# Cross-attention and FFN in one kernel: the maxima's short key chunk moved out of the key loop and rewritten as four full-array matmuls

## The chip, the core and the metric

The program runs on one core of one Trainium2 chip. The metric is the device time of one execution in microseconds. TensorE is called PE (PEld for its weight loads), VectorE DVE, ScalarE ACT, GpSimd POOL and SyncE SP, as in the profile. Two kinds of float are used on PE: float32, whose matmul stands in the trace as two instructions (two passes), and the rounded float32r, with one.

## The reference

A block with cross-attention and a feed-forward network, batch 1, everything in float32:

```python
x = x + xattn(layernorm(x), ctx)      # 2048 rows of 256; ctx 1601 rows of 192
#   q = layer_norm(x, g) @ Wq         # 16 heads of 64
#   k, v = split(ctx @ Wkv); a learned null key and value is put in front: 1602 keys
#   attn = softmax(mask(q k^T / 8)); out = layer_norm((attn v) @ Wout, g_out)
x = x + ffn(layernorm(x))             # 256 -> 1024 -> 1024 -> 256, weights +-1, relu
```

## The kernel before, in words

The attention is cut into 32 units `(p, b)`: a pair `p` of heads (8 of them, two heads of 64 fill the 128 partitions) and a block `b` of 512 query rows (4). The order of all instructions on every engine is the program's order; it is written by hand (`manual_schedule`), and nothing is moved by a scheduler. Buffers come from rings: a new tile of a ring takes the place of the one allocated so many allocations earlier, and its first writer waits for that one's last reader.

Two rings hold PSUM. `spare` (tag "s", two buffers) holds the scores of the even and the odd key tile, the weighted sum `av` and the output projection `po`. `flex` (tag "f", two buffers) holds the maxima's products, the denominators `den`, the turned maxima `mt`, and the projections of queries, keys and values (`psq`, `psk`, `psv`).

The softmax needs a row maximum before the exponentials are taken. It is computed from rounded copies: `qr` and `kr` are float32r copies of the queries `qT` and keys `kT`. A unit's maxima are found one unit ahead, in `max_chunk(p, b, n)`: for each of 4 query tiles of 128 rows there are three wide chunks of 512 keys (n = 0 to 11), each two matmuls, one for each head on its 64 rows of the array (L400) and one DVE reduction over both (L403). The keys 1536 to 1601, 66 of them, are the short chunk, `REST` (n = 12): for all four query tiles and both heads eight matmuls of 66 columns on 64 rows (L384) and one reduction (L387) into column 3 of the tile `mx`.

One unit in the order of PE:

1. The loop over 13 key tiles. Step k: `exps` issues the scores of tile k (two float32 matmuls on 64 rows each, four instructions, L442), for k below 2 also the matmul that adds the shift (L466), and ACT takes the exponential (L468) into the tile `e`; then one chunk of the next unit's maxima. The chunks go in the order 0 to 10, REST, 11, so REST is in step 11. POOL adds up the `e` tiles into `acc` for the denominators (L720, L722, L728).
2. `den`: the denominators of the unit before (L499; in 28 of the units ahead of the weighted sum, in units 1, 30 and 31 within it, in unit 0 not at all), whose reciprocal (L511) and copies (L517, ACT) give `aoT`.
3. The weighted sum `av`, 13 times four matmuls with 32 columns of weights (L475), copied to `avs` by ACT (L782).
4. The projections: `mt` (L413) turns the next unit's maxima, DVE makes the shift `mT` of them (L415); `po` is the output projection of the unit before (L488), added to `y_sb` by DVE (L493); `psq` the queries two units ahead (L211), copied by ACT to `qr` and `qT` (L212, L213); then, for seven pairs out of eight, a half of the next pair's keys (`project_k`, L270 and L275, in b = 0 and 1) or values (`project_v`, L305 and L320, in b = 2 and 3). DVE makes `kT` of the key projection (L232), ACT rounds it to `kr` (`round_k`, L289, ahead of `avs`), and copies the values (L329).

The prologue computes the first pair's keys, values and the maxima of unit (0, 0), with POOL rounding the keys; its REST comes after the query projection of unit (0, 1). After the attention the feed-forward part follows; its first block starts beside the last unit.

Of the kernel before, what the change touches and what calls it, by code (L numbers as in the profile page):

```python
# [31 lines left out]
REST = 12  # L32
# [6 lines left out]
def xattn_ffn(ctx, tc, x, ctxT, mask, g_norm, null_kv, wq, wkv, wout, g_out, k0, k1, k2, s0, s1, s2, out):  # L39
# [9 lines left out]
    def flex(name):  # L49
        return ps_f.tile([128, 2, 512], F32, tag="f", name=name)  # L50
# [97 lines left out]
    with ExitStack() as att:  # L148
# [15 lines left out]
        spent = ap.tile([128, 1], F32, name="spent")  # L164
        ones_r = ap.tile([128, 128], F32R, name="ones_r")
        mcol = ap.tile([128, 128], F32, name="mcol")
        pick = ap.tile([128, 4, 1], F32, name="pick")

        weights = {}
# [25 lines left out]
        def project_q(p, b, get=flex, part=None):  # L195

            if part is not None:
                if part == 0:
                    halves["q"] = get(f"psq_{p}_{b}")
                ps = halves["q"]  # L200
                nc.tensor.matmul(
                    ps[:, 0, :], weights[p][0][:, part, :], xnT[:, b, part, :], start=part == 0, stop=part == 1
                )
                if part == 0:
                    return
            qT = wp.tile([128, 512], F32, tag="qT", name=f"qT_{p}_{b}")
            qr = wp.tile([128, 512], F32R, tag="qr", name=f"qr_{p}_{b}", bufs=1)
            if part is None:
                ps = get(f"psq_{p}_{b}")
            for c in range(2) if part is None else ():  # L210
                nc.tensor.matmul(ps[:, 0, :], weights[p][0][:, c, :], xnT[:, b, c, :], start=c == 0, stop=c == 1)  # L211
            nc.scalar.mul(qr, ps[:, 0, :], DH**-0.5)  # L212
            nc.scalar.mul(qT, ps[:, 0, :], DH**-0.5)  # L213
            queries[p, b] = (qT, qr)
# [19 lines left out]
        def first_keys(n, get, part=None):  # L234

            kT, _, kr = pairs[0]
            chunks = (CHUNKS[1], CHUNKS[2]) if n == 1 else (CHUNKS[n],)
            if part != 1:
                halves["k"] = get(f"psk_0_{n}")
            ps = halves["k"]  # L240
            for i, (start, w) in enumerate(chunks):
                if part is None or part == i:
                    nc.tensor.matmul(
                        ps[:, i, :w], weights[0][1][:, 0, :], ctx_a[:, ds(start, w)], start=True, stop=False
                    )
            if part == 0:
                return
            for i, (start, w) in enumerate(chunks):
                rows = ts(i, 64)
                nc.tensor.matmul(  # L250
                    ps[:, i, :w], weights[0][2][rows, 0, :], ctx_b[rows, ds(start, w)], start=False, stop=True
                )
            for i, (start, w) in enumerate(chunks):
                for part in range(2 if n == 0 else 1):
                    keys = ds(256 * part, 256) if n == 0 else ds(start, w)
                    relative(kT, ps[:, i, ts(part, 256)] if n == 0 else ps[:, i, :w], keys)
                    if n == 0 and part == 0:
                        nc.scalar.copy(kr[:, keys], kT[:, keys])
                    else:
                        nc.gpsimd.tensor_copy(kr[:, keys], kT[:, keys])  # L260
            if n == 3:
                nc.vector.memset(kT[:, KEYS:], 0.0)

        def project_k(p, m):

            kT = pairs[p][0]
            start, w = HALF_KEYS[m]
            ps = flex(f"psk_{p}_{m}")
            for i in range(2):
                nc.tensor.matmul(  # L270
                    ps[:, i, :w], weights[p][1][:, 0, :], ctx_a[:, ds(start + i * w, w)], start=True, stop=False
                )
            for i in range(2):
                rows = ts(i, 64)
                nc.tensor.matmul(  # L275
                    ps[:, i, :w], weights[p][2][rows, 0, :], ctx_b[rows, ds(start + i * w, w)], start=False, stop=True
                )

            for i in range(2):
                relative(kT, ps[:, i, :w], ds(start + i * w, w))  # L280
            if m == 1:
                nc.vector.memset(kT[:, KEYS:], 0.0)

        def round_k(p, m):

            kT, _, kr = pairs[p]
            start, w = HALF_KEYS[m]
            keys = ds(start, 2 * w)
            nc.scalar.copy(kr[:, keys], kT[:, keys])  # L289

        def keys_stepped(p):

# [83 lines left out]
        def max_chunk(p, b, n, get=flex):  # L376
            ps = get(f"max_{p}_{b}_{n}")
            qr, kr = queries[p, b][1], pairs[p][2]
            if n == REST:
                start, w = CHUNKS[3]  # L380
                for t in range(4):
                    for j in range(2):
                        rows = ts(j, DH)
                        nc.tensor.matmul(  # L384
                            ps[:, j, ts(t, w)], qr[rows, ts(t, 128)], kr[rows, ds(start, w)], start=True, stop=True
                        )
                nc.vector.tensor_reduce(  # L387
                    maxima[p, b][:, :, :, 3].rearrange("p t j -> p j t"),
                    ps[:, :, : 4 * w].rearrange("p j (t k) -> p j t k", k=w),
                    AX.X,  # L390
                    ALU.max,
                )
                return
            t, c = divmod(n, 3)
            if n == 0:
                maxima[p, b] = wp.tile([128, 4, 2, 4], F32, tag="mx", name=f"mx_{p}_{b}")
            start, w = CHUNKS[c]
            for j in range(2):
                rows = ts(j, DH)
                nc.tensor.matmul(  # L400
                    ps[:, j, :w], qr[rows, ts(t, 128)], kr[rows, ds(start, w)], start=True, stop=True
                )
            nc.vector.tensor_reduce(maxima[p, b][:, t, :, c], ps[:, :, :w], AX.X, ALU.max)  # L403
# [33 lines left out]
        def scores(p, b, k, ps):  # L437
            kT, qT = pairs[p][0], queries[p, b][0]
            n = rows_of(k)
            for j in range(2):  # L440
                rows = ts(j, DH)
                nc.tensor.matmul(  # L442
                    ps[:n, j, :],
                    kT[rows, ds(128 * KEY_TILES[k], n)],
                    qT[rows, :],
                    start=k < 2,
                    stop=k >= 2,
                    skip_group_check=k >= 2,
                )
# [111 lines left out]
                nc.vector.tensor_scalar_mul(xnT[:, b, 1, :], pts[1][:, 1, :], gn_sb[:, 1:2])  # L561

        units = [(p, b) for p in range(NP) for b in range(NB)]
        order = (*range(REST - 1), REST, REST - 1)

        begin = tc.manual_schedule()
        begin.__enter__()
# [51 lines left out]
        for j in range(2):  # L619
            nc.gpsimd.dma_start(out=nullv[:, ts(j, DH)], in_=null_kv[1:2, :])  # L620
        nc.gpsimd.memset(mcol, 0.0)
        nc.gpsimd.memset(kept, 0.0)
        nc.gpsimd.tensor_scalar(ones_r, ident, 0.0, 1.0, ALU.mult, ALU.add)
        nc.gpsimd.tensor_tensor(pick[:, :, 0], ident[:, 0:4], ident[:, DH : DH + 4], ALU.add)
# [41 lines left out]
        input_turned(1, spare)  # L666
        max_chunk(0, 0, 8)
        max_chunk(0, 0, 11)
        project_q(0, 1, spare)
        max_chunk(0, 0, REST)  # L670
        odd = spare("sT_0_0_1")
        sT = [spare("sT_0_0_0"), odd]
        scores(0, 0, 1, sT[1])
        max_combined(0, 0)
        max_turned(0, 0)
        scores(0, 0, 0, sT[0])
        masked_counted(flex)
        begin.__exit__(None, None, None)
        last = None
        with tc.manual_schedule():  # L680
            for u, (p, b) in enumerate(units):
# [27 lines left out]
                for k in range(KC):  # L709
                    if k == (2 if 2 < u < len(units) - 4 else 8) and last is not None:  # L710
                        nc.scalar.copy(seen[:, 1:2], last[3][:1, 0, 0:1])
                    if k == 0 and u > 0:

                        odd = spare(f"sT_{p}_{b}_1")
                        sT = [spare(f"sT_{p}_{b}_0"), odd]
                    es.append(exps(p, b, k, sT))
                    if nxt is not None:
                        max_chunk(*nxt, order[k])
                    if k == 2:
                        nc.gpsimd.tensor_tensor(acc, es[1], es[2], ALU.add)  # L720
                    elif 2 < k < 8:
                        nc.gpsimd.tensor_tensor(acc, acc, es[k], ALU.add)  # L722
# [64 lines left out]
                    max_turned(*nxt)  # L787
                if nxt is None:
                    uT = turned(0)
                if last is not None:  # L790
                    project_out(*last[:2], aoT)
                if u + 2 < len(units):
                    project_q(*units[u + 2])
                if p + 1 < NP:

                    (project_k if b < 2 else project_v)(p + 1, b % 2)
                    if b == 2:
                        keys_stepped(p + 1)
                last = (p, b, avs, acc)
# [154 lines left out]
```

## Time and profile before

| What | Value |
|---|---|
| median of 3 runs (lowest to highest) | 1270.56 us (1269.84 to 1270.65) |
| the profiled execution's own time | 1270.18 us |
| its span | 1268.4 us |
| granted TensorE clock | 1.00 |
| wide chunk's reduction on DVE, L403, 384 of them | 1218 ns each |
| exponential on ACT, L468, 416 of them | 1024 ns each |
| wide chunk's matmuls on PE, L400 | 280.6 us busy |
| short chunk's matmuls on PE, L384 | 29.6 us busy |
| weighted sum on PE, L475 | 363.6 us busy |
| PE in one unit's loop, 399.1 to 413.3 us of the span | 14.20 us busy of 14.20 |

The first exponentials of most units follow each other after 32.85 us (33.5 where a unit projects the first half of the values, 31.2, 31.0 and 30.0 in the last pair). Times are those of one execution; the profile numbers lines by kernel.py. Single records of the trace are meant where a time has three digits after the point.

### The profile page before, as it was taken

To read this page: it belongs to the slowest core of one execution; us is meant where nothing else is said; L and a number is where in the kernel's file an instruction comes from. 1 tells how busy PE (TensorE), PEld (TensorE's weight loads), DVE (VectorE), ACT (ScalarE), POOL (GpSimd) and SP (SyncE) were. 2 spreads that over 40 slices of the span, in tenths; PEclk is the share of its full clock that TensorE was granted. 3 is DMA by queue.
4 is the path that set the end of the run, shared out by engine and by line. 5 is a ranking of instruction groups with operands and counts; after the bars stand their busy time and mean duration, and the time that the engine had idled before them with its cause. 6 is when DMAs were issued, how large, how long until landed. Compare 5 with 4: busy or idle time off the path is not lost.

```text
span 1268.4 us, 19642 instructions
## 1 busy us (share of the span) xinstructions
PE 1257.9 (99%) x8332; PEld 644.0 (51%) x8332; DVE 761.7 (60%) x812; ACT 717.9 (57%) x982; POOL 1008.5 (80%) x515
## 2 busy tenths in 40 slices
PE   8999999999999999999999999999999999999998
PEld 5344444444444444444444444444444443788887
DVE  6687766656665566556655666656666793635431
ACT  4776666666666656665666566666666676322120
POOL 5898999899889988998899988998898999701100
PEclk9999999999999999999999999999999999999999
DMA  6000000000000000000000000000000010000000
GB/s 171 1 1 5 1 1 13 5 1 1 13 5 1 1 14 5 1 1 13 5 1 2 13 5 1 1 1 6 1 17 1 1 42 1 1 17 1 17 17 17
DMA packets 16984, 13.46 MB, mean 11 GB/s; under 512 B 3152, under 2 KB 16336, under 8 KB 16896
## 3 DMA queue, kind: packets, MB, share of 16 engines
q1 hardware_dynamic: 15904, 11.21, 3.2%
q8 instruction: 65, 1.06, 0.4%
q10 hardware_dynamic: 656, 0.79, 0.2%
q0 software_dynamic: 336, 0.21, 0.1%
q14 instruction: 23, 0.19, 0.0%
HBM read 10.11 MB, written 2.10 MB: 10 GB/s over the span
## 4 chain that ended last, share of the span: by engine, by line
PE 95%; POOL 2%; ACT 1%; DMA 1%; issue 0%; DVE 0%; SPq 0%; DVEq 0%; POOLq 0%; ACTq 0%
PE sT L442 28%; PE av L475 27%; PE ps L836 12%; PE max L400 7%; PE psq L211 4%; PE po L488 4%; PE ps L867 2%; PE psv L305 2%; PE psk L270 1%; PE den L499 1%; PE sT L466 1%; PE psv L320 1%; POOL acc L728 1%; PE psk L275 1%; PE max L384 1%; PE mt L413 1%
## 5 line engine op out<-in xcount | busy, mean ns | idle before, releaser
L403 DVE TENSOR_REDUCE mx<-max 128x2 f32<-128x1024 f32 x384 | 444.4, 1218 | 86.0 <-PE max L400 82.3
L728 POOL TENSOR_TENSOR acc<-acc,e 128x1024 f32<-128x1024 f32 x192 | 473.1, 2464 | 15.1
L468 ACT ACTIVATE e<-sT 128x1024 f32<-128x1024 f32 x416 | 425.8, 1024 | 87.7 <-PE sT L466 44.3
L442 PE MATMUL sT<-qT,kT 64*128 64x512 f32 x1664 | 444.8, 608 | 1.6 <-ACT e L468 1.3
L722 POOL TENSOR_TENSOR acc<-acc,e 128x1024 f32<-128x1024 f32 x160 | 379.3, 2371 | 12.6
L475 PE MATMUL av<-e,v 128*32 128x512 f32 x3328 | 363.6, 592 | 0.1
L400 PE MATMUL max<-kr,qr 64*128 64x512 f32 x768 | 280.6, 718 | 1.2 <-ACT qr L227 1.0
L475 PEld LDWEIGHTS av<-e,v 128*32 128x32 f32 x3328 | 107.4, 110 | 237.9 <-issue 230.1
L442 PEld LDWEIGHTS sT<-qT,kT 64*128 64x128 f32 x1664 | 134.0, 185 | 132.6 <-ACT e L468 121.0
L720 POOL TENSOR_TENSOR acc<-e,e 128x1024 f32<-128x1024 f32 x32 | 75.6, 2363 | 59.6 <-ACT e L468 59.6
L400 PEld LDWEIGHTS max<-kr,qr 64*128 64x128 f32 x768 | 76.7, 187 | 88.6 <-DVE mx L403 65.2
L517 ACT COPY aoT<-r 32x256 f32<-32x256 f32 x224 | 90.2, 403 | 33.4 <-DVE r L511 31.1
L782 ACT COPY avs<-av 128x512 f32<-128x512 f32 x32 | 18.8, 587 | 145.8 <-PE av L475 145.8
L415 DVE TENSOR_TENSOR mT<-mt,pick 128x512 fp32r<-128x512 f32 x32 | 22.1, 690 | 113.4 <-PE mt L413 112.9
L518 DVE TENSOR_TENSOR aoT<-avs,aoT 128x512 f32<-128x512 f32 x28 | 33.3, 1189 | 94.4 <-ACT aoT L517 94.4
L836 PE MATMUL ps<-h0hi,w 128*128 128x512 f32 x256 | 79.6, 392 | 0.0
L836 PE MATMUL ps<-h0lo,w 128*128 128x512 f32 x256 | 78.9, 389 | 0.0
L124 POOL TENSOR_TENSOR y_sb<-y_sb,gout_sb 128x256 f32<-128x256 f32 x12 | 9.3, 777 | 85.6 <-DVE y_sb L91 85.6
L824 ACT ACTIVATE h1hi<-ps 128x1024 fp32r<-128x1024 f32 x16 | 16.4, 1027 | 99.2 <-PE ps L836 99.2
L212 ACT ACTIVATE qr<-psq 128x512 fp32r<-128x512 f32 x31 | 18.5, 598 | 93.5 <-PE psq L211 91.4
L488 PE MATMUL po<-wo,aoT 128*128 128x256 f32 x256 | 60.5, 379 | 0.0
L825 DVE SCALAR_TENSOR_TENSOR h1lo<-ps,h1hi 128x1024 fp32r<-128x1024 f32 x16 | 19.6, 1224 | 67.0 <-ACT h1hi L824 67.0
(171 smaller groups left out, 1207.8 us busy)
## 6 DMA issues: line engine op xcount, KB each, us to landing
out_x<-o SPq DMA_DIRECT2D x7, 256.0 KB, 2.1
x_sb<-in_x SPq DMA_DIRECT2D x3, 512.0 KB, 5.2
wa<-in_wkv SPq DMA_DIRECT2D x8, 128.0 KB, 2.9
wb<-in_wkv SPq DMA_DIRECT2D x16, 64.0 KB, 2.5
wq<-in_wq SPq DMA_DIRECT2D x8, 128.0 KB, 2.2
wo<-in_wout SPq DMA_DIRECT2D x8, 128.0 KB, 2.1
xnT<-in_k SPq DMA_DIRECT2D x1, 1024.0 KB, 5.7
ctx_a<-in_ctxT SPq DMA_DIRECT2D x2, 256.0 KB, 6.2
```

Of the source, the lines that this page charges most:

```text
L211: nc.tensor.matmul(ps[:, 0, :], weights[p][0][:, c, :], xnT[:, b, c, :], start=c == 0, stop=c == 1)
L400: nc.tensor.matmul(ps[:, j, :w], qr[rows, ts(t, 128)], kr[rows, ds(start, w)], start=True, stop=True)
L403: nc.vector.tensor_reduce(maxima[p, b][:, t, :, c], ps[:, :, :w], AX.X, ALU.max)
L442: nc.tensor.matmul(ps[:n, j, :], kT[rows, ds(128 * KEY_TILES[k], n)], qT[rows, :], start=k < 2, stop=k >= 2, skip_group_check=k >= 2,)
L468: nc.scalar.activation(e, ps, AF.Exp)
L475: nc.tensor.matmul(av[ts(i, 32), 0, :], v[:n, KEY_TILES[k], ts(i, 32)], e[:n, i // 2, :], start=k == 1, stop=k == 0, tile_position=(0, 32 ...
L488: nc.tensor.matmul(pv[:, t, :], aoT[:, ts(t, 128)], weights[p][3], start=True, stop=True)
L517: nc.scalar.copy(aoT[ds(64 * j + 32 * rows, 32), ts(h, 256)], r[ds(64 * j + 32 * h, 32), :])
L720: nc.gpsimd.tensor_tensor(acc, es[1], es[2], ALU.add)
L722: nc.gpsimd.tensor_tensor(acc, acc, es[k], ALU.add)
L728: nc.gpsimd.tensor_tensor(acc, acc, es[k], ALU.add)
L836: nc.tensor.matmul(ps[:, f, :], w(c)[:, ts(2 * g + f, 128)], parts[part][:, c, :], start=i == 0, stop=i == len(steps) - 1,)
```

## The change

REST is computed differently and elsewhere. The last 66 keys of the two heads are kept apart in a tile of their own, block-diagonal: head 0's in rows 0 to 63 of the first 66 columns, head 1's in rows 64 to 127 of the other 66, zeros elsewhere. One matmul on the whole array then gives both heads' products for a query tile, 132 columns, and four do the work of the eight. Two such tiles, one for even and one for odd pairs, are zeroed once by POOL; ACT fills them after `round_k` (POOL in the prologue), with two copies of 64x66, and `round_k` leaves those keys out.

REST of unit u + 2 now stands at the end of unit u, behind the query projection that it needs, and the reduction of it with it; the prologue does it for the first two units. From unit 2 on, the query projection is put ahead of the output projection, and REST behind the latter; in units 0 and 1 REST stands between the two parts of the key projection. In the loop, step 1 has no maxima any more, and steps 2 to 12 have the chunks 1 to 11 (step 0 keeps chunk 0).

```diff
+        apart = [ap.tile([128, 2, KEYS - CHUNKS[3][0]], F32R, name=f"apart_{i}") for i in range(2)]
...
             start, w = HALF_KEYS[m]
-            keys = ds(start, 2 * w)
+            keys = slice(start, min(start + 2 * w, CHUNKS[3][0]))
             nc.scalar.copy(kr[:, keys], kT[:, keys])
+            if m == 1:
+                keys_apart(p, nc.scalar.copy)
+
+        def keys_apart(p, copy):
+
+            start, w = CHUNKS[3]
+            for j in range(2):
+                copy(apart[p % 2][ts(j, DH), j, :], pairs[p][0][ts(j, DH), ds(start, w)])
...
             if n == REST:
-                start, w = CHUNKS[3]
+                w = 2 * CHUNKS[3][1]
                 for t in range(4):
-                    for j in range(2):
-                        rows = ts(j, DH)
-                        nc.tensor.matmul(
-                            ps[:, j, ts(t, w)], qr[rows, ts(t, 128)], kr[rows, ds(start, w)], start=True, stop=True
-                        )
+                    nc.tensor.matmul(
+                        ps[:, t // 2, ts(t % 2, w)],
+                        qr[:, ts(t, 128)],
+                        apart[p % 2].rearrange("p j k -> p (j k)"),
+                        start=True,
+                        stop=True,
+                    )
                 nc.vector.tensor_reduce(
-                    maxima[p, b][:, :, :, 3].rearrange("p t j -> p j t"),
-                    ps[:, :, : 4 * w].rearrange("p j (t k) -> p j t k", k=w),
+                    maxima[p, b].rearrange("p (i t) j c -> p i (t j) c", i=2)[:, :, :, 3],
+                    ps[:, :, : 2 * w].rearrange("p i (t k) -> p i t k", k=w // 2),
...
+        for i in range(2):
+            nc.gpsimd.memset(apart[i].bitcast(F32), 0.0)
...
         max_chunk(0, 0, 11)
+        max_chunk(0, 0, REST)
         project_q(0, 1, spare)
-        max_chunk(0, 0, REST)
...
         max_turned(0, 0)
+        max_chunk(0, 1, REST)
         scores(0, 0, 0, sT[0])
...
                     es.append(exps(p, b, k, sT))
-                    if nxt is not None:
-                        max_chunk(*nxt, order[k])
+                    if nxt is not None and k != 1:
+                        max_chunk(*nxt, max(k - 1, 0))
...
+                if u >= 2 and u + 2 < len(units):
+                    project_q(*units[u + 2])
                 if last is not None:
                     project_out(*last[:2], aoT)
-                if u + 2 < len(units):
+                if u < 2:
                     project_q(*units[u + 2])
+                if u + 2 < len(units) and u >= 2:
+                    max_chunk(*units[u + 2], REST)
                 if p + 1 < NP:
 
-                    (project_k if b < 2 else project_v)(p + 1, b % 2)
+                    if u < 2:
+                        project_k(p + 1, b, 0)
+                        max_chunk(*units[u + 2], REST)
+                        project_k(p + 1, b, 1)
+                    else:
+                        (project_k if b < 2 else project_v)(p + 1, b % 2)
```

The remaining lines split `project_k` into the two parts named above and, in the prologue's `first_keys`, replace POOL's one rounding copy of the last keys by `keys_apart(0, nc.gpsimd.tensor_copy)`.

More of the change, by code (lines that the diff above doesn't have):

```diff
@@ L256, in first_keys @@
                     relative(kT, ps[:, i, ts(part, 256)] if n == 0 else ps[:, i, :w], keys)
-                    if n == 0 and part == 0:
+                    if n == 3:
+                        keys_apart(0, nc.gpsimd.tensor_copy)
+                    elif n == 0 and part == 0:
                         nc.scalar.copy(kr[:, keys], kT[:, keys])
@@ L262, in first_keys, with project_k @@
                 nc.vector.memset(kT[:, KEYS:], 0.0)
-        def project_k(p, m):
+        def project_k(p, m, part=None):
             kT = pairs[p][0]
             start, w = HALF_KEYS[m]
-            ps = flex(f"psk_{p}_{m}")
-            for i in range(2):
+            if part != 1:
+                halves["k"] = flex(f"psk_{p}_{m}")
+            ps = halves["k"]
+            for i in range(2) if part != 1 else ():
                 nc.tensor.matmul(
@@ L272, in project_k @@
                 )
+            if part == 0:
+                return
             for i in range(2):
@@ L378, in max_chunk @@
             qr, kr = queries[p, b][1], pairs[p][2]
+            if (p, b) not in maxima:
+                maxima[p, b] = wp.tile([128, 4, 2, 4], F32, tag="mx", name=f"mx_{p}_{b}")
             if n == REST:
-                start, w = CHUNKS[3]
+                w = 2 * CHUNKS[3][1]
                 for t in range(4):
-                    for j in range(2):
-                        rows = ts(j, DH)
-                        nc.tensor.matmul(
-                            ps[:, j, ts(t, w)], qr[rows, ts(t, 128)], kr[rows, ds(start, w)], start=True, stop=True
-                        )
+                    nc.tensor.matmul(
[5 more added lines that the diff above has]
+                    )
                 nc.vector.tensor_reduce(
-                    maxima[p, b][:, :, :, 3].rearrange("p t j -> p j t"),
-                    ps[:, :, : 4 * w].rearrange("p j (t k) -> p j t k", k=w),
+                    maxima[p, b].rearrange("p (i t) j c -> p i (t j) c", i=2)[:, :, :, 3],
+                    ps[:, :, : 2 * w].rearrange("p i (t k) -> p i t k", k=w // 2),
                     AX.X,
@@ L394, in max_chunk @@
             t, c = divmod(n, 3)
-            if n == 0:
-                maxima[p, b] = wp.tile([128, 4, 2, 4], F32, tag="mx", name=f"mx_{p}_{b}")
             start, w = CHUNKS[c]
@@ L563, in xattn_ffn @@
         units = [(p, b) for p in range(NP) for b in range(NB)]
-        order = (*range(REST - 1), REST, REST - 1)
         begin = tc.manual_schedule()
```

## The prediction

> **What bounds the kernel now.** I read the page first (engine shares, the chain that ended last), then the groups by form, then the timeline around one loop end, single records of the trace where the timeline merges too much, and last the one unit that computes no maxima.
>
> ```profile
> PE 1257.9 (99%) x8332; PEld 644.0 (51%) x8332; DVE 761.7 (60%) x812; ACT 717.9 (57%) x982; POOL 1008.5 (80%) x515
> PE 95%; POOL 2%; ACT 1%; DMA 1%; issue 0%; DVE 0%; SPq 0%; DVEq 0%; POOLq 0%; ACTq 0%
> ```
>
> Of the groups by form, the two of the short chunk (instructions, then busy us and mean ns of one):
>
> ```profile
> L384 PE MATMUL max<-kr,qr 64*128 64x66 f32 x256 | 29.6, 351 | 0.0
> L387 DVE TENSOR_REDUCE mx<-max 128x8 f32<-128x528 f32 x32 | 22.7, 709 | 0.7 <-PE max L384 0.5
> ```
>
> PE never rests and carries the chain; the short chunk, REST below, is 29.6 us on PE, so that is the most that its removal could bring. PE's busy share hides waits, since a matmul's record runs through its own start-up, so starts decide:
>
> ```profile
> 409.72 1.02 PE L442 MATMUL sT<-qT,kT 64*128 64x512 f32 x4
> 410.17 0.80 PE L400 MATMUL max<-kr,qr 64*128 64x512 f32 x2
> 410.81 1.09 PE L442 MATMUL sT<-qT,kT 64*128 64x512 f32 x4
> 411.33 0.93 PE L384 MATMUL max<-kr,qr 64*128 64x66 f32 x8
> 411.73 0.42 PEld L384 LDWEIGHTS max<-kr,qr 64*128 64x128 f32 x6 [0.24 <-issue]
> 412.09 1.11 PE L442 MATMUL sT<-qT,kT 64*128 64x512 f32 x4
> 412.30 0.71 DVE L387 TENSOR_REDUCE mx<-max 128x8 f32<-128x528 f32 x1
> 412.63 0.80 PE L400 MATMUL max<-kr,qr 64*128 64x512 f32 x2
> 413.36 0.16 PEld L499 LDWEIGHTS den<-acc,ones 128*32 128x32 f32 x8 [0.56 <-issue]
> ```
>
> Steps come every 1.09 and 1.16 us by turns (409.72 to 410.81), a pair in 2.25. That pair is a latency circle over the two score buffers: exp 1.02, 0.05 until the next score's weight load, 0.11 load, two passes of 0.43, 0.21 until the next exp: 2.25. A wide maximum (0.21 of PE) fits into its slack. The unit without maxima proves it: its thirteen exps span 13.82 us, the others' 13.89.
>
> ```profile
> 1055.22 0.30 PEld L442 LDWEIGHTS sT<-qT,kT 64*128 64x128 f32 x4 [1.02 <-ACT e L468]
> 1056.20 0.30 PEld L442 LDWEIGHTS sT<-qT,kT 64*128 64x128 f32 x4 [0.69 <-ACT e L468]
> ```
>
> There, with PE free, score weights still wait for ACT. Outside the loop no such slack exists: the projections stand back to back.
>
> ```profile
> 391.74 1.89 PE L488 MATMUL po<-wo,aoT 128*128 128x256 f32 x8
> 393.47 1.88 PE L211 MATMUL psq<-xnT,wq 128*128 128x512 f32 x4
> 395.19 1.95 PE L305 MATMUL psv<-wa,ctx_a 128*128 128x128 f32 x16
> ```
>
> **The change, part by part.** The sum is against the profiled execution, 1270.18 us (span 1268.4 and 1.8 around it), which is 0.38 below the median 1270.56.
>
> *REST leaves the loop.* REST holds PE from 411.73 to the next score's real start at 412.18 (its second weight load in the single records): 0.45. A wide chunk would have released PE at 411.95 and the exp circle allows 411.97, so REST lengthens the loop by 0.21 only. ACT agrees: the last exp starts 1.305 after the one before, where the alternation gives 1.095.
>
> *The other chunks shift by a step, none at k=1.* The first key tile still carries chunk 0, so the second exp starts as before. Without a maximum at k=1 the next score could start 0.1 earlier, but its exp would stand behind ACT's previous one, which already ends back to back (starts 1.094 apart for 1.02 of work). Worth nothing. DVE, 1.131 per wide reduction back to back, gets a free step there; it does not set the loop either, so again nothing.
>
> *The denominators' buffer.* This is a wait that the diff does not name. `den` takes the flexible buffer used two allocations earlier. Before, that was REST's, whose short reduction ended at 412.30 + 0.71 = 413.01, hidden: the weights of `den` went out at 413.36, 0.11 after the last maximum left the array. After, it is a wide chunk's. Its matmuls end on PE at 412.12; DVE starts at 412.20 to 412.23 (0.06 to 0.10 later, or behind the reduction begun at 411.10), takes 1.214, ends at 413.42 to 413.44, and PE passes a semaphore 0.04 + 0.05 later: 413.53, that is 0.17 after the old start. Queued behind on PE are `den` and the whole weighted sum. So 28 units (those with `den` ahead of the weighted sum) lose 0.17 in place of gaining 0.21: +4.8. Three units (0, 1 and 30) go straight to the weighted sum and gain: -0.6. If the wait fell elsewhere the 28 would gain 5.9; I take the loss, since the order of allocation leaves no other buffer.
>
> *REST among the projections.* Four full-array matmuls of 132 columns instead of eight half-array ones of 66. The eight ran in pairs 7 ns apart, pairs 0.11 apart, with only some 0.03 of columns each: weight loads set the pace. Full-array loads of 128 columns pace alike: the value projection's matmuls (L305) come every 0.112. I take four such slots, 0.45, because loads cannot run further ahead than one and the next projection's first load joins the row. Low end: 132 columns at the 0.21 per 512 of the wide chunk, 0.055 each, 0.22. High end: the price of a float32 matmul of this width, two passes at L488's 0.216 per 256 columns, 0.22 each, 0.89; against it, the columns of the old REST took no visible time beside its loads. Nothing below zero, since no PE work is dropped there. Thirty units: +13.5, between +6.6 and +26.7.
>
> A page would make it cheaper. The Trainium skill, "TensorE: Matmul & The Clock Gate", section "Back-to-back issue gap", gives about 81 ns per matmul for a stream of load and matmul pairs at 128 columns; L305's 112 ns in this trace disagree, and the measurement decides. By the page these thirty units would cost an estimated 9.7 us and the whole sum would be about 14.6.
>
> *Query projection ahead of the output projection.* Both full-array, 1.72 and 1.73, so the exchange costs nothing, and it hides the copies of `qr` and `qT` (1.3 us after the projection ends) under `po`. Without that cover REST would wait 1.3 in each unit. `po` moves 1.7 later: its DVE addition (1.22) ends about 1.4 after it, while the score that takes its buffer comes over 1.8 after it even where no key or value projection follows. The weight DMAs that SP holds until `psq` and `po` are read move by the same 1.7, a unit ahead of use. On DVE, REST's reduction (0.71) stands between that addition and the keys' subtraction (0.63 twice), which waits for key matmuls 2.2 us long: hidden; uncovered it is 0.71 per unit with keys.
>
> *Copies.* Two 64x66 copies for each of seven pairs on ACT ahead of `avs`, where ACT idles 4.41: nothing; uncovered, 14 times 0.17 to 0.4 (smallest copy, and L517), 2 to 6 us. On POOL one more small copy (0.24) and two memsets at the start.
>
> *Prologue.* The query projection, begun at 28.76, now stands behind a REST that waits for a buffer until about 29.7; the transpose at 32.50 moves to 32.8; the second REST waits for `qr`, whose projection ended 1.4 later, and stands in front of the score begun at 32.73. The first exp (34.65) comes 0 to 1 later; I take +0.7.
>
> Sum: 13.5 + 4.8 - 0.6 + 0.7 = +18.4 on 1270.18, or 1289.0 by the median.
>
> **Rivals.** *Faster: DVE's queue sets the loop.* For it: steps of 1.127 lie within 0.004 of DVE's 1.131. Then leaving REST's reduction out of the loop saves 0.63 (0.71 less the 0.08 by which reductions overlap) against 0.45 outside: -0.18 in 30 units, 1265. Against it: the unit without maxima is no shorter, and score loads wait for ACT. It decides from the point where a loop step follows DVE's end, and no such wait shows. Equally below zero would be a load price under 0.21.
>
> *`den` does not wait.* Then +13.5 - 6.5 + 0.7 = +7.7: 1278. Against it: all 28 event records of L499 come 0.04 after the end of a reduction.
>
> *Slow columns in full-array form*, 0.89 a unit: +31.6, 1302. No row shows a short matmul of that type on the full array.
>
> *It does nothing*, REST on PE at 0.22 with `den` not waiting: +0.8, 1271.
>
> **How the numbers follow.** My forecast has 0.73 (30 times 0.40 to 0.50, 28 times 0.11 to 0.20, -0.6 and a prologue of 0 to 1: +14.5 to +21, so 1285 to 1292). `den` not waiting 0.10; slow columns 0.05; the faster rival 0.08; nothing 0.04. The range takes in the forecast's bounds and the 1278 case: 1276 to 1293, leaving out 0.17. About 0.2% (2.5 us) is what a measurement of this kernel can tell. Faster by more 0.08, same 0.04, slower 0.88.
>
> **What the profile would show.** Right: `den` loads waiting for a DVE reduction in 28 units, about 0.17 later against the last exp's old place; the last exp 1.10 after the one before; REST in slots of 0.11 between output and key or value projection; units of 32.85 near 33.5. Wrong: loop steps below 1.12; REST's slots near 0.06 or 0.22; no DVE wait at `den`; a score waiting for `po`'s addition.

## The result and the profile after

| | before | after |
|---|---|---|
| median (lowest to highest) | 1270.60 us (1269.84 to 1270.65) | 1290.09 us (1289.76 to 1290.17) |
| the profiled execution's own time, and its span | 1270.18, 1268.4 us | 1290.05, 1288.3 us |
| granted TensorE clock | 1.00 | 1.00 |

Before stands here with one more run than in the table above. The ratio is 1.015, with a 95% interval of 1.0135 to 1.0166: slower by 19.5 us.

First the page of after: busy time of each engine, and the shares of the chain that ended last.

```profile
PE 1267.3 (98%) x8204; PEld 661.0 (51%) x8204; DVE 761.7 (59%) x812; ACT 717.7 (56%) x996; POOL 1008.6 (78%) x518
PE 74%; DVE 23%; ACT 1%; DMA 1%; issue 0%; SPq 0%; DVEq 0%; POOL 0%; ACTq 0%
```

PE has 128 matmuls fewer and is busy 9.4 us longer. The new thing is DVE with 23% of the chain, where it had none. The chain itself, over one unit (start, us, what), shows where that comes from:

```profile
411.12 10.28 DVE mx L421 x9
421.40 0.14 issue
421.54 0.64 PE den L517 x8
422.18 11.16 PE av L493 x104
...
435.31 1.73 PE po L506 x8
437.04 0.40 PE max L400 x4
437.44 1.16 PE psv L321 x10
```

This must be read with care. Followed back from `den` the chain reaches a wide reduction (L421), and then the eight before it, since they stand back to back. That `den` waits for DVE is real. That the nine reductions set the pace of the loop does not follow: they start 1.131 apart (419.046, 420.177, 421.308), while the maxima's matmuls ahead of them start 1.158 and 1.095 apart by turns (418.129, 419.287, 420.382), as the exps do, and e6 below relieves DVE and gains nothing. The last line but one is REST in its new place: 0.40 of the chain, with nothing beside it.

The timeline of after at the end of the loop (start, us, engine, line, operation; in brackets the idle time before and what ended it):

```profile
420.38 0.80 PE L418 MATMUL max<-kr,qr 64*128 64x512 f32 x2
421.51 0.19 PEld L517 LDWEIGHTS den<-acc,ones 128*32 128x32 f32 x8 [0.96 <-issue]
421.54 0.64 PE L517 MATMUL den<-acc,ones 128*32 128x256 f32 x8 [0.35 <-DVE mx L421]
```

All 28 of these waits, from the answer for line L517 (us, times):

```profile
  DVE mx L421: 9.8, 28
```

In single records the reduction of chunk 10 ends at 421.392, PE's event follows at 421.431, the load at 421.507 and the first matmul of `den` at 421.537. The first exp of the unit starts at 407.371: `den` starts 14.166 after it, where before it was 13.950 (unit 11 in both). The 0.35 of idle time per wait is counted from 421.182, the end of the last maximum's record, and such ends are modelled by the profile: without a wait, the load of `den` came 0.07 ahead of that end (413.363 for 413.435 in before). So the wait is 0.43 long; 0.21 of it uses up the loop's gain, and the rest is the later start.

The groups by form show the short chunk (instructions, then busy us and mean ns of one), and after them the timeline of the projections:

```profile
L400 PE MATMUL max<-apart,qr 128*128 128x132 f32 x128 | 23.6, 306 | 1.0 <-DVE mx L421 1.0
L407 DVE TENSOR_REDUCE mx<-max 128x8 f32<-128x528 f32 x32 | 22.4, 700 | 5.3 <-PE max L400 5.3
```

```profile
433.43 1.88 PE L213 MATMUL psq<-xnT,wq 128*128 128x512 f32 x4
435.15 1.89 PE L506 MATMUL po<-wo,aoT 128*128 128x256 f32 x8
435.35 0.60 ACT L214 ACTIVATE qr<-psq 128x512 fp32r<-128x512 f32 x1 [1.37 <-PE psq L213]
...
436.69 0.75 PE L400 MATMUL max<-apart,qr 128*128 128x132 f32 x4
...
437.28 1.32 PE L321 MATMUL psv<-wa,ctx_a 128*128 128x128 f32 x10
438.22 0.70 DVE L407 TENSOR_REDUCE mx<-max 128x8 f32<-128x528 f32 x1
```

REST's busy time fell from 29.6 to 23.6 us, and the kernel is slower all the same. In single records its four matmuls start at 436.690, 436.938, 437.052 and 437.161 and the value projection at 437.277; the loads run 0.11 apart. `qr` is ready at 435.95, so nothing waits for it.

Differences between the first exps of following units put the time in its places: 1.34 us before the first exp (36.00 for 34.65), 0.36, 0.29 and 0.63 in units 0 to 2, 0.67 in each of the 25 units 3 to 27 (16.7), 0.38 and 0.59 in units 28 and 29, -0.20 in unit 30, and -0.2 behind the last first exp: 19.9, the difference of the spans. Of the 1.34, some 0.21 lies ahead of anything that the change moves (e9). In unit 28 `den` came as late before (14.335 after the first exp, now 14.319), so REST's price is left there almost alone.

### The profile page after: what moved, and what is told of

It is laid out like the page before. It is cut to its first block, busy times and chain, and to the rows that moved or that the text cites. A ratio compares the mean times of both kernels' runs of the same rounds, so it can differ in the third digit from the quotient of the medians.

```text
span 1288.3 us, 19431 instructions
## 1 busy us (share of the span) xinstructions
PE 1267.3 (98%) x8204; PEld 661.0 (51%) x8204; DVE 761.7 (59%) x812; ACT 717.7 (56%) x996; POOL 1008.6 (78%) x518
## 4 chain that ended last, share of the span: by engine, by line
PE 74%; DVE 23%; ACT 1%; DMA 1%; issue 0%; SPq 0%; DVEq 0%; POOL 0%; ACTq 0%
PE av L493 28%; DVE mx L421 22%; PE sT L460 11%; PE ps L865 11%; PE po L506 4%; PE psq L213 4%; PE ps L896 2%; PE max L418 2%; PE psv L321 2%; PE psk L276 2%; PE den L517 1%; PE sT L484 1%; PE psv L336 1%; PE max L400 1%; PE psk L283 1%; DMA x_sb<-in_x 1%
## 5 line engine op out<-in xcount | busy, mean ns | idle before, releaser
L421 DVE TENSOR_REDUCE mx<-max 128x2 f32<-128x1024 f32 x384 | 444.4, 1219 | 73.7 <-PE max L418 71.6
L418 PE MATMUL max<-kr,qr 64*128 64x512 f32 x768 | 291.6, 751 | 1.2 <-ACT qr L229 1.0
L493 PEld LDWEIGHTS av<-e,v 128*32 128x32 f32 x3328 | 127.2, 110 | 218.1 <-issue 210.8
L511 DVE TENSOR_TENSOR y_sb<-po,y_sb 128x1024 f32<-128x1024 f32 x28 | 34.3, 1224 | 68.2 <-PE po L506 68.2
```

Source lines behind the costliest of these rows:

```text
L418: nc.tensor.matmul(ps[:, j, :w], qr[rows, ts(t, 128)], kr[rows, ds(start, w)], start=True, stop=True)
L493: nc.tensor.matmul(av[ts(i, 32), 0, :], v[:n, KEY_TILES[k], ts(i, 32)], e[:n, i // 2, :], start=k == 1, stop=k == 0, tile_position=(0, 32 ...
```

## The experiments

The theory is the prediction's: REST costs its four weight loads where PE has no slack, `den` waits for the buffer of a wide chunk, and the loop gains 0.21. The rivals: DVE's queue sets the loop, the columns rather than the loads set REST's price, and the form rather than the place is to blame. Every experiment was timed in several rounds against the kernel before on the same chip, except e9.

### e1 and e2: is the wait at `den` real, and what is it worth?

```diff
-                if quarters:
-                    den = flex(f"den_{p}_{b}")[:, 0, :256]
-                    denominators(last[3], den)
-                    aoT = divided_quarters(*last[:3], den)
...
+                    if k == 2 and quarters:
+                        den = flex(f"den_{p}_{b}")[:, 0, :256]
+                        denominators(last[3], den)
+                        aoT = divided_quarters(*last[:3], den)
```

`den` goes behind the first two tiles of the weighted sum, in e1 on the kernel after, in e2 on the kernel before.

> The changed kernel with the denominators' matmuls put behind the first two key tiles of the weighted sum (as units 1, 30 and 31 have them already) instead of ahead of it; nothing else differs. Theory (in the changed kernel these matmuls stand and wait for the reduction of the last but one wide chunk): two tiles are 0.86 us of PE work and cover the wait, so 28 units lose the 0.215 by which the denominators start later than before and gain the 0.21 that the loop is shorter: 28 x 0.425 = 11.9 us less, about 1278.2, and no wait of the denominators for a reduction. Rival (the later start is a drain of the array or a later exponential, and would only move to the weighted sum): within 2 us of 1290.

> The kernel before with the same displacement of the denominators, as the control: there their buffer was the short chunk's, read early. Theory: no wait to cover, 1269.5 to 1271.5. Rival (taking the denominators off the loop's end is worth something by itself): as much faster as the other run, down to 1259.

e1: 1278.09 us, ratio 1.0059 (1.0044 to 1.0074), 12.0 below after. e2: 1270.22, ratio 0.9998 (0.9989 to 1.0007). The timeline of e1 at the end of the loop:

```profile
417.16 1.92 PE L493 MATMUL av<-e,v 128*32 128x512 f32 x16
418.90 0.61 PE L517 MATMUL den<-acc,ones 128*32 128x256 f32 x8
```

No wait of `den` for DVE is left; all idle time ahead of its line in that kernel's answer for L517 (us, times) is

```profile
  issue: 16.8, 56
```

The first load of the weighted sum, at 417.162, comes 0.071 ahead of the modelled end of the last maximum (417.233), as that of `den` did before the change. The unit takes 33.09, 0.43 less than after: the 0.215 by which `den` was late, and the 0.21 that the shorter loop now gives (28 times 0.43 is 12.0). The loop itself is as long as in after, 13.68. On the kernel before the same edit is worth nothing, so it cures only the wait that the change made.

### e3: what does REST cost in its new place?

```diff
-                for t in range(4):
+                for t in (*range(4), *range(4)):
```

On the kernel after, REST's four matmuls are issued twice into the same places; all values stay as they are.

> The changed kernel with the short chunk's four full-array matmuls issued twice into the same places (the second time gives the same values). Theory (PE takes them at the pace of weight loads, 0.11 each, in a stretch without slack): 30 x 4 x 0.112 = +13.4 and 0.5 to 0.9 in the prologue, about 1304. Rival, columns hidden and loads cheap (the 0.66 per unit that the changed kernel lost is the wait alone): +2 or less, 1290 to 1292. Rival, slow columns: +26, 1316.

1304.11 us, ratio 1.0263 (1.0246 to 1.0280): 14.0 above after, or 0.44 for each of 32 sets. Units take 33.96 (+0.44). So the price is four slots of 0.11. By the page that the prediction weighed (the Trainium skill, "TensorE: Matmul & The Clock Gate", section "Back-to-back issue gap") a set would be an estimated 0.32, and this run 1300.5; the row of the value projection was the better guide.

### e4: the new place with the old form

On the kernel after, REST stands where the change puts it, but as the eight half-array matmuls of before, reading `kr`; the tiles `apart` and their copies are left out.

```diff
-                w = 2 * CHUNKS[3][1]
+                start, w = CHUNKS[3]
...
+                    for j in range(2):
+                        rows = ts(j, DH)
+                        nc.tensor.matmul(
+                            ps[:, j, ts(t, w)], qr[rows, ts(t, 128)], kr[rows, ds(start, w)], start=True, stop=True
+                        )
```

> The changed kernel with the short chunk in its old form (eight matmuls of 66 columns on half the rows, from the rounded keys; no separate key tiles, copies and memsets) at its new place. Theory: four pairs at the pace of weight loads cost the same 0.45, and two changes between whole-array and half-array matmuls come on top, at about 0.1 each in 28 units: 1290 to 1296. Rival (the full-array form is what costs): under 1284.

1298.35 us, ratio 1.0219 (1.0204 to 1.0234): 8.3 above after, and above the range expected. Its timeline:

```profile
437.92 1.89 PE L493 MATMUL po<-wo,aoT 128*128 128x256 f32 x8
439.74 0.63 PE L391 MATMUL max<-kr,qr 64*128 64x66 f32 x8
440.31 1.38 PE L310 MATMUL psv<-wa,ctx_a 128*128 128x128 f32 x10
```

The four pairs are 0.11 apart as ever, with 66 columns where the full-array matmuls have 132, so the columns do not set that pace; but the unit is 0.31 longer (33.83 for 33.52). In single records the last matmul of `po` starts at 439.434, and REST's first weights are loaded at 439.741, 0.307 later; in after they are loaded 0.001 after that matmul's start. A gap comes back behind REST, where the last pair starts at 440.10 and the value projection's first load is at 440.305. Both loads come 0.07 ahead of the modelled end of the matmul before them (439.813 and 440.376). In all 28 units with REST behind `po` it is so, and in before at all 28 loads of `den`: where the form changes, the next weights are loaded only about when the last matmul's record ends. A change between the half array and the whole one costs 0.155 here, as the mean of the two. The Trainium skill, "TensorEngine Tiling (Array Packing)", section "Key Properties", says that a change of the tiling mode drains TensorE; these runs agree, and 0.155 is its price here.

### e8: the new form in the old place

On the kernel after, all orders and the prologue are those of before; REST is in step 11 of the loop as four full-array matmuls on `apart`.

```diff
+        order = (*range(REST - 1), REST, REST - 1)
...
-                    if nxt is not None and k != 1:
-                        max_chunk(*nxt, max(k - 1, 0))
+                    if nxt is not None:
+                        max_chunk(*nxt, order[k])
```

> The changed kernel's full-array form and separate key tiles at the old place in the loop (step 11, old order of the chunks and of the projections, the prologue's order as before). Theory: four loads pace it at 0.45 as the eight half-array ones did, and going from half-array to whole-array matmuls and back costs 0.31 (the price that the half form had among the whole-array projections): 31 x 0.31 = 9.6, about 1280. Rival (the form itself is the gain, and the place the loss): 1269 or less.

1280.68 us, ratio 1.0077 (1.0062 to 1.0092). Its timeline around step 11:

```profile
414.80 1.09 PE L460 MATMUL sT<-qT,kT 64*128 64x512 f32 x4
415.82 0.66 PE L400 MATMUL max<-apart,qr 128*128 128x132 f32 x4
416.41 1.13 PE L460 MATMUL sT<-qT,kT 64*128 64x512 f32 x4
```

From score to score it is 1.61 us, where it was 1.28 (410.81 to 412.09) with the half-array form. The last exp of the loop starts 1.652 after the one before it (1.305 before the change): 0.35 for two changes of the array. The profile puts the idle time ahead of REST's first load, 0.76, down to a DVE reduction, but that one ended at 415.170, long before the load at 415.816. The load comes 0.07 ahead of the modelled end of the last score (415.887), as in e4. Form and place belong together: the new form is dearer in the loop, the old one is dearer outside it.

### e5 and e6: the order of the chunks alone, on the kernel before

```diff
-        order = (*range(REST - 1), REST, REST - 1)
+        order = tuple(range(KC))
```

```diff
-        order = (*range(REST - 1), REST, REST - 1)
+        order = (0, REST, *range(1, REST))
```

e5 (first edit) puts REST last, so that the second to last allocation ahead of `den` is a wide chunk's. e6 (second edit) puts REST, in its old form, into step 1, with `den` behind the first two tiles of the weighted sum as in e2.

> The kernel before with only the last two chunks exchanged (wide chunk 11 in step 11, the short chunk in step 12), so that the denominators take a wide chunk's buffer with nothing moved out of the loop. Theory (the wait comes from whose buffer it is): denominators 0.2 later against the unit's first exponential, as in the changed kernel, 28 x 0.215 = 6.0; the three units without that wait gain 0.21 and lose 0.24 of PE: about 1276.5. Rival (the later denominators of the changed kernel come from the chunks' shift or the missing chunk in step 1): PE's work alone, +0.03 a unit, 1270 to 1272.

> The kernel before with the short chunk, in its old form, moved to step 1 of the loop and the wide chunks 1 to 11 to steps 2 to 12, and the denominators behind two key tiles of the weighted sum. Theory (the loop is a circle of scores and exponentials; the short chunk's 0.45 on PE overruns the 0.15 that PE has free in step 1, and the even scores carry the rest, about 0.2, to the end of the loop): no gain, 1269 to 1272. Rival (DVE's queue sets the loop, so an early short reduction shortens it): 0.2 a unit less, 1263 to 1265.

e5: 1276.73 us, ratio 1.0047 (1.0032 to 1.0062). Its waits at L499, and its timeline:

```profile
  DVE mx L403: 6.4, 28
```

```profile
415.03 0.93 PE L384 MATMUL max<-kr,qr 64*128 64x66 f32 x8
416.20 0.64 PE L499 MATMUL den<-acc,ones 128*32 128x256 f32 x8 [0.24 <-DVE mx L403]
```

One line of order makes the wait: `den` starts 14.17 after the first exp, and the units take 33.08 (+0.23; 28 times that is 6.4, and 6.3 was measured). Nothing else of the change is in this kernel.

e6: 1270.47 us, ratio 0.9998 (0.9989 to 1.0007). The 0.21 of REST moves from the end of the loop to the third exp (1.313 instead of 1.094 after the second), and the loop stays at 13.90. From step 2 on DVE has 0.5 us less queued than in before (a reduction of 0.71 in place of 1.21), and the pace stays 1.09 and 1.16 by turns. With DVE setting the loop this kernel would have been 5 to 7 us faster: that rival falls.

### e7: the cover of the copies

```diff
-                if u >= 2 and u + 2 < len(units):
-                    project_q(*units[u + 2])
...
-                if u < 2:
+                if u + 2 < len(units):
```

On the kernel after, `po` stands ahead of `psq` again, and REST directly behind `psq`.

> The changed kernel with the output projection ahead of the query projection again, as before, so that the short chunk directly follows the projection whose copy it reads. Theory: it waits for both copies of the queries, 1.3 us after the projection leaves PE, in 28 units: +36, 1324 to 1328; if it waits for the rounded copy alone, 0.8 each, 1313. Rival (the copies are early enough, the exchange of the two projections was not needed): 1289 to 1291.

1317.74 us, ratio 1.0369 (1.0351 to 1.0386): 27.7 above after, between the two expectations. Its timeline:

```profile
447.09 0.60 ACT L214 ACTIVATE qr<-psq 128x512 fp32r<-128x512 f32 x1 [3.09 <-PE psq L213]
...
447.74 0.67 PE L400 MATMUL max<-apart,qr 128*128 128x132 f32 x4 [0.69 <-ACT qr L214]
```

REST waits for `qr` alone and starts 0.05 after that copy ends; the copy to `qT` (L215, begun at 447.58) is still running then. Units take 34.51, 0.99 more than after. So the exchange of the two projections hides 0.99 per unit, not 1.3; the expectation by `qr` alone (1313) falls short by 0.17 a unit, which was not taken apart.

### e9: the prologue, a single execution

```diff
-        max_chunk(0, 0, REST)
         project_q(0, 1, spare)
+        max_chunk(0, 0, REST)
...
-        max_chunk(0, 1, REST)
         scores(0, 0, 0, sT[0])
         masked_counted(flex)
+        max_chunk(0, 1, REST)
```

On the kernel after, REST of unit (0, 0) goes behind the query projection, as in before, and REST of unit (0, 1) behind the first unit's scores and the counting of masked keys.

> The changed kernel with the prologue's two short chunks put elsewhere: the first behind the query projection of the second unit, as before, the second behind the first unit's scores and the count of masked keys. Theory (the changed prologue is late because the first one holds up that projection until a buffer is free, and the second stands in front of the first scores): the first exponential at about 35.0 us in place of 36.0, the rest of the profile alike, 1289. Rival (POOL's two more copies and memsets make it late): still 35.8 to 36.0.

One execution gave 1289.44 us, beside 1270.31 for the kernel before. The first exp starts at 35.46, between the 35.0 expected and the rival's 35.8, and 0.54 earlier than in after. But the start of the program varies from one execution to the next, and part of such a difference comes from there. The reduction of chunk 11 of unit (0, 0) stands ahead of everything that is moved; it starts at 29.584 in before, 29.796 in after and 30.071 in e9, and in the other traces anywhere from 29.35 (e2) to 30.89 (e7). From that start to the first exp it is 5.07 in before (5.06 in e2, e5 and e6, which share its prologue), 6.20 in after (6.20 in e1 and e7) and 5.39 in e9. So the changed prologue costs 1.13, and e9 gives back 0.81 of it.

In before the query projection starts at 28.76, in after at 30.50, behind this pair:

```profile
30.03 0.64 PE L400 MATMUL max<-apart,qr 128*128 128x132 f32 x4 [1.04 <-DVE mx L421]
30.50 1.93 PE L213 MATMUL psq<-xnT,wq 128*128 128x512 f32 x4
```

and in e9 at 29.24. There the other REST stands in front of the matmul that adds the shift:

```profile
34.34 0.65 PE L400 MATMUL max<-apart,qr 128*128 128x132 f32 x4
34.92 0.50 PE L484 MATMUL sT<-mT,ones_r 64*128 64x512 f32 x2
```

Counted from the same reduction, `mt` is turned after 2.91 in before, 3.62 in after and 2.74 in e9; from there to the first exp it is 2.15, 2.58 and 2.65. So the first REST's place costs 0.71 in after and the second's 0.42, and the 0.32 left in e9 is the price of the second one's new place. For the rival, POOL's additional work, no sign is seen: the reduction of chunk 11, behind most of that work, starts at 29.61 to 30.89 in the six kernels with it and at 29.35 to 30.21 in the five without, ranges that overlap and so do not exclude a small effect.

## Why the prediction was right

Time and direction: 1289.0 was predicted, 1290.09 measured, and each of its four terms is found in its place. The sum of +18.4 stands against 19.9 in the profiled executions; nearly all of the difference is in `den` and the prologue, both sized too low.

- *REST among the projections, 0.45 a unit, 13.5 in all.* Measured: 0.44 by e3. The loads set its pace, as the row of the value projection had it (e4 has the same 0.11 with half the columns); neither the low end (0.22) nor the high end (0.89) is seen.
- *`den` waits for a wide chunk.* Shown from three sides: the 28 waits in after, their going in e1, and their coming in e5 with nothing but the order changed. The size was a little low: 0.215 instead of 0.17 a unit, 6.0 instead of 4.8 for 28 units (in unit 28 it cost nothing, as said above). The term that was mis-sized is the way from the reduction's end to the first matmul: 0.145, not 0.04 + 0.05, since the load follows the event's record only after another 0.025 and the matmul 0.03 after that. The old price of the event was taken from a place where it was hidden.
- *The loop gains 0.21.* 13.68 instead of 13.89; the last exp is 1.095 after the one before, as forecast. The gain is lost to the wait in 28 units: e1 shows it once the wait is gone.
- *The free step is worth nothing.* The second exp of the free step does come earlier, 1.002 after its neighbour instead of 1.094, and the third is 1.251 later instead of 1.159: the sum is the same.
- *Three units gain 0.21.* Unit 30 did (-0.20). Units 0 and 1 hold REST too and came out at +0.36 and +0.29, where 0.45 less 0.21 would be 0.24. The loop of unit 0 became only 0.14 shorter (from its first exp's start to its last one's end 14.63 for 14.77), that of unit 1 0.22; so outside the loop both lost 0.5, some 0.06 more than REST's 0.44, which was not taken apart.
- *The prologue, +0.7, at most 1.* This step failed on size: the first exp came 1.34 later, and 1.13 later counted from the work ahead of the change (e9). REST was taken to hold the query projection until 29.7, and the transpose to slip by 0.3. It held it until 30.50, and the transpose, which stands behind that projection, slipped by 0.71 by the same count; the second REST took 0.42. e9 gives back 0.81 of the 1.13.
- *The covers.* The copies of `qr` and `qT` lie under `po`: without that cover 0.99 a unit (e7), where the prediction had 1.3, since REST waits for `qr` alone. REST's reduction delayed nothing that the trace shows, and the addition of `po` one score load by 0.7, as it did before.

Of the rivals, the faster one (DVE sets the loop) falls by e6, where relief of DVE leaves the loop's length and pace as they were. "`den` does not wait" is e1's kernel in effect: 1278.09 for the 1278 worked out. Slow columns fall by e3, and so does a REST at 0.22.

No kernel that was run beats the one before. e6, the old form in step 1 with `den` moved as in e2, ties with it at 1270.47: REST has its cheapest place in the loop, where it costs 0.21 of its 0.45.

## What to carry to other kernels

Work in a loop that waits on a latency circle costs only what it overruns; moved to a stretch where its engine runs back to back it costs all of its time, even if its busy time in the profile has become shorter (29.6 to 23.6 us here). When the order of allocations in a ring changes, ask whose buffer the next tile takes: here a tile with a short reader gave way to one with a long reader, and one line of order cost 6.3 us, which two tiles of later work in front of the waiting one hide. A matmul's form belongs to its neighbours: half-array among half-array, full among full.

## What the runs showed of the hardware that was not expected

- A change between half-array and full-array matmuls costs 0.155 (e4) to 0.17 (e8, 0.35 for two): the next form's first weights are loaded 0.203 (e4, behind REST) to 0.518 (e8, behind a score) after the start of the last matmul of the other form, each time 0.07 ahead of its modelled end, where between matmuls of one form they come 0.001 after that start (after). That is more than a whole short matmul (0.11).
- A rounded matmul of 132 columns on the whole array costs no more than a pair of 66 columns on its two halves: 0.11, the pace of their weight loads, in both.
- A wait that a matmul really stands in costs more than the event's own records: 0.145 from the end of the reduction to the first matmul.
